# The layout of the attention output in HBM, and the tiles and queues of the first head's convolution

## The chip, the cores and the metric

The kernel runs on one core of one Trainium2 chip. The metric is the device time of one launch in microseconds (us). Three runs of the kernel before gave 3805.25, 3806.37 and 3806.59 us; the median is 3806.37. The trace and all rows quoted below come from one further, profiled execution.

The engines are called PE (TensorE), DVE (VectorE), ACT (ScalarE), POOL (GpSimd) and SP (SyncE). SP, ACT and POOL issue transfers, each in the order of its own instructions: SP and ACT through hardware queues (q1 and q10 in the profile), POOL through the software queue (q0).

## What is computed

Two layers over an image `x` of 48 channels and 256 by 256 pixels, in float32. Layer 0 is an attention over patches: 4 by 4 pixels are one token, so there are 4096 tokens (and a border of zero tokens), and each of 8 heads has 96 rows (6 channels of 16 pixels).

```python
def _L0_conv_ref(x, w_qkv, w_dw, temperature, w_proj):
    qkv = jnp.einsum('bchw,oc->bohw', x, w_qkv)
    qkv = dwconv3x3(qkv, w_dw)
    q, k, v = jnp.split(qkv, 3, axis=1)
    q, k, v = (heads(q), heads(k), heads(v))      # unfold into patches, 8 heads
    q = _l2norm(q)
    k = _l2norm(k)
    attn = jnp.einsum('bhcn,bhcm->bhnm', q, k) * temperature
    attn = jax.nn.softmax(attn, axis=-1)
    out = jnp.einsum('bhcn,bhnm->bhcm', v, attn)
    out = fold(out.reshape(b, -1, out.shape[-1]), h, w)
    return jnp.einsum('bchw,oc->bohw', out, w_proj)

x = x + _L0_conv_ref(_gn(x), ...)                 # _gn: normalisation over groups of channels
x = x + _L1_conv_ref(_gn(x), Ws, Hs, Cs, 64)      # three products over W, H and C in windows of 64 by 64
```

## The kernel before

The work runs in this order.

1. *Statistics and pointwise product.* `x` is read into 96 partitions (two halves of the image, 48 channels each), 16 rows at a time, by loads `xr` on SP and ACT. DVE takes statistics, PE forms q, k and v of the first two heads, and they go to HBM (`t1`).
2. *Convolution of the first head* (`depthwise_first`). The image is cut into ten rows of strips (`CR + 1`), and a `Depthwise` object does one of them for seven strips at once: 126 partitions (7 strips of 18 channels) by 4 rows of 256 pixels. The objects go in pairs: the second of a pair forms its taps on PE (L223), the first on DVE (L234). Then come square (ACT L245), sum (DVE L249), the sum over channels (PE L253), a root, the scaled result `o` (DVE L279), its high part `oh` (ACT L288) and the rest `ol` (POOL L292). `store` (L297) writes these three to `qkv` in HBM. One store has 504 KB: from each of 126 partitions 4 KB, to 16 rows of 256 bytes in HBM. All 30 are issued by POOL. The tiles come from a pool of two buffers each (`bufs` is 2), and the padded input `pad` from twice as many; `pad` loads are issued by SP. When a buffer is taken again, the instruction that writes it waits until the store that reads it has landed.
3. *Attention*, head by head, in an order written out by hand. First the eight key tiles of head 0 are loaded (`load_key`, L313), alternately from SP and ACT; a key tile of 512 columns takes four transfers, and eight where it crosses the border of a strip (576 columns). They wait for all stores of head 0's `qkv`. `scores` forms logits on PE (L339) into one of three `big` buffers of PSUM, ACT takes the exponential (L541), `weigh` multiplies with the values (L570) and DVE adds up `oacc`. The convolution of the next head runs beside it, one row for each group of queries. At the end of a head `store` (L590) turns the result by PE into `oo`, 96 rows by 512 tokens (two buffers), and POOL writes it into `os_`, which lies in HBM as 768 rows (48 channels by 16 places in the patch) of 4096 tokens.
4. *Projection.* It goes by eight tiles `t`, each of 256 tokens (16 image rows) in both halves of the image. For each half SP loads `pot` (L709), 48 partitions by 16 places by 256 tokens, and `pxt` (L710), the same pixels of `x`: four loads of 768 KB in the order pot, pxt, pot, pxt. PE multiplies with the projection weights (L715), DVE adds to `pxt` (L722) and takes statistics (L726), and POOL writes the sum to `x1s` in HBM (L731). The tiles have three buffers.
5. *Layer 1* reads `x1s` in windows and writes the output.

In step 2 the instructions of an engine are put in order by a scheduler; in step 3's loop they stand as written. The loads ahead of that loop:

```python
load_query(0, 0)
for m in range(NM):
    load_key(0, m, nc.scalar if m % 2 else nc.sync)
for m in range(2):
    load_value(0, m)
    turn(0, m)
```

Of the kernel before, what the change touches and what calls it, by code (L numbers as in the profile page):

```python
# [8 lines left out]
F32 = mybir.dt.float32  # L9
# [7 lines left out]
C = 48  # L17
# [3 lines left out]
KS = 4  # L21
KK = KS * KS
NH = 8
HD = C * KK // NH
NT = (H // KS) * (W // KS)
# [7 lines left out]
PX = W // KS  # L33
# [2 lines left out]
M1 = (NH - H0) * HC  # L36
GROUPS = [(0, H0), (H0, NH)]
NOT = 3
T3 = 3
WS = 64  # L40

# [2 lines left out]
def conv_preact_kernel(  # L44
# [15 lines left out]
    nc = tc.nc  # L60
# [4 lines left out]
    dram = ctx.enter_context(tc.tile_pool(name="dram", bufs=1, space=DRAM))  # L65
# [6 lines left out]
    CN = CR * PX  # L72
    t1 = [dram.tile([(h1 - h0) * HC, TR, W + 2], F32, name=f"t1_{h0}") for h0, h1 in GROUPS]
    qkv = [dram.tile([3, CH, HC * KK, CN + PX], F32, name=f"qkv{h}") for h in range(NH)]
    os_ = dram.tile([C * KK, NT], F32, name="os_")
    x1s = dram.tile([C, H, W], F32, name="x1s")


# [14 lines left out]
    for s in range(2):  # L93
        r = slice(s * C, (s + 1) * C)
        for h in range(NH if s == 0 else H0):
            o = s * M0 + h * HC if h < H0 else (h - H0) * HC
            nc.scalar.dma_start(
                out=(wq[r] if h < H0 else wr[0:C])[:, o : o + HC].rearrange("c (z e) -> c z e", z=3),
                in_=w_qkvT.rearrange("c (z h e) -> h c z e", z=3, h=NH)[h],
# [68 lines left out]
    class Strip:  # L168
# [24 lines left out]
        def store(self):  # L193
            for s, rows in enumerate(both_halves(t1[1], 2 * self.j, 2, base=1)):
                nc.sync.dma_start(out=rows, in_=self.ot[:, 2 * s : 2 * s + 2, :])

    class Depthwise:


        def __init__(self, h, r, pool=None):  # L200
            self.h, self.r = h, r
            self.pool, self.bufs = (pool, 2) if pool else (cv, 1)

        def load(self):
            g = [i for i, (h0, h1) in enumerate(GROUPS) if h0 <= self.h < h1][0]
# [85 lines left out]
            self.ol = self.pool.tile([NP1, KK, PX], F32R, name="ol", tag="t4", bufs=self.bufs)  # L291
            eng.tensor_sub(self.ol, self.o, self.oh.bitcast(F32))  # L292

        def store(self, parts=(0, 1, 2)):
            px = slice(self.r * PX, (self.r + 1) * PX)
            for i in parts:
                nc.gpsimd.dma_start(  # L297
                    out=qkv[self.h][i].rearrange("j (c k) n -> (j c) k n", k=KK)[:, :, px],
                    in_=self.o if i == 2 else (self.ol if i else self.oh).bitcast(F32),
                )  # L300
# [59 lines left out]
    def depthwise_first():  # L360

        with tc.tile_pool(name="dg", bufs=1) as dg, tc.tile_pool(name="dps", bufs=3, space=PSUM) as dps:
            diag = dg.tile([NP1, 9, NP1], F32, name="diag")
            for t in range(9):
                nc.gpsimd.tensor_scalar_mul(diag[:, t, :], ident[:NP1, :NP1], dwt[:, 0, t : t + 1])
            rows = [Depthwise(0, r, dg) for r in range(CR + 1)]
            for d in rows[:2]:
                d.load()
            for i in range(0, CR + 1, 2):
                a, b = rows[i : i + 2]  # L370
                b.taps_on_tensor(diag, dps.tile([NP1, 2, 512], F32, name="dps"))
                a.first()
                for t in range(1, 9):
                    a.tap(t)
                for d in rows[i + 2 : i + 4]:
                    d.load()
                for d in (a, b):
                    d.square()
                    d.reduce()
                    d.norm()  # L380
                    d.root(on_scalar=True)
                    d.scale()
                    d.high()
                    d.low(nc.gpsimd)
                    d.store()


    with tc.tile_pool(name="xn", bufs=1) as xnp, tc.tile_pool(name="cst", bufs=1) as cst, tc.tile_pool(
        name="nps", bufs=2, space=PSUM
# [9 lines left out]
        for j in range(0, HALF, LR):  # L399
            for s in range(2):  # L400
                eng = nc.sync if s == 0 else nc.scalar
                eng.dma_start(
                    out=xr[s * C : (s + 1) * C, j : j + LR, :], in_=xc[:, s * HALF + j : s * HALF + j + LR, :]
# [8 lines left out]
        for g, (w, k) in enumerate(((wq, P2), (wr, C))):  # L412
            m = w.shape[1]
# [31 lines left out]
        for y in range(0, HALF, OR):  # L445
            ot = xnp.tile([2 * M0, OR, W + 2], F32, name="ot0", bufs=4)
# [9 lines left out]
    cv = attention.enter_context(tc.tile_pool(name="cv", bufs=1))  # L456
# [8 lines left out]
    with tc.If(nc.values_load(large) > 0):  # L465
# [8 lines left out]
        with tc.tile_pool(name="mk", bufs=NM) as mk, tc.tile_pool(name="mq", bufs=2) as mq, tc.tile_pool(  # L474
            name="mps", bufs=2, space=PSUM
# [23 lines left out]
    with tc.tile_pool(name="ahead", bufs=2) as ah, tc.tile_pool(name="ae", bufs=3) as ae, tc.tile_pool(  # L499
        name="asm", bufs=6  # L500
# [6 lines left out]
        def load_key(h, m, eng=nc.sync):  # L507
            keys[h, m] = ah.tile([128, 2, 512], F32R, name="kt", bufs=14)
            load_keys(keys[h, m], h, m, eng)
# [73 lines left out]
        def store(h, m):  # L583

            pt = one.tile([HD, 4, 128], F32, name="pt", tag="one")
            for i in range(4):
                nc.tensor.transpose(pt[:, i, :], oaccs[h, m // 2][:, m % 2, i * HD : (i + 1) * HD], ident)  # L587
            oo = asm.tile([HD, 512], F32, name="oo", bufs=2)
            nc.scalar.copy(oo, pt.rearrange("p i n -> p (i n)"))  # L589
            nc.gpsimd.dma_start(out=os_[h * HD : (h + 1) * HD, m * 512 : (m + 1) * 512], in_=oo)  # L590

        load_query(0, 0)
        for m in range(NM):
            load_key(0, m, nc.scalar if m % 2 else nc.sync)
        for m in range(2):
            load_value(0, m)
            turn(0, m)
# [9 lines left out]
        with tc.manual_schedule():  # L607
            load_query(0, 1)
            block = scores(0, 0)
            for h in range(NH):  # L610
                more = h + 1 < NH
                rows = {r: Depthwise(h + 1, r) for r in range(CR + 1)} if more else {}
                for g in range(NG):
                    p, d, n = rows.get(g - 2), rows.get(g - 1), rows.get(g)
# [42 lines left out]
                    for k in range(NK):  # L657
                        s = (h * NG + g) * NK + k
# [33 lines left out]


    l1c = ctx.enter_context(tc.tile_pool(name="l1c", bufs=1))
    RP = 16
    NP = RP // KS * (W // KS)
    with tc.tile_pool(name="pj", bufs=3) as pj, tc.tile_pool(name="pjs", bufs=1) as pjs, tc.tile_pool(
        name="pps", bufs=3, space=PSUM
    ) as pps, tc.tile_pool(name="pp1", bufs=1, space=PSUM) as pp1:
        st1 = pjs.tile([P2, HALF * W // 512, 6], F32, name="st1")  # L700
        ov = os_.rearrange("(c k) n -> c k n", k=KK)
        for t in range(HALF // RP):
            ot = pj.tile([P2, KK, NP], F32, name="pot")
            xt = pj.tile([P2, RP, W], F32, name="pxt")
            for s in range(2):
                r = slice(s * C, (s + 1) * C)
                n0 = s * (NT // 2) + t * NP
                y0 = s * HALF + t * RP
                nc.sync.dma_start(out=ot[r], in_=ov[:, :, n0 : n0 + NP])  # L709
                nc.sync.dma_start(out=xt[r], in_=xc[:, y0 : y0 + RP, :])  # L710
            xv = xt.rearrange("p (py ki) (px kj) -> p ki kj py px", ki=KS, kj=KS)
            for ki in range(KS):
                ps = pps.tile([P2, KS, NP], F32, name="pps")
                for i in range(0, KS, 2):
                    nc.tensor.matmul(  # L715
                        ps[:, i : i + 2, :],
                        lhsT=wp,
                        rhs=ot[:, ki * KS + i : ki * KS + i + 2, :],
                        start=True,
                        stop=True,  # L720
                    )
                nc.vector.tensor_add(  # L722
                    xv[:, ki], ps.rearrange("p k (py px) -> p k py px", py=RP // KS), xv[:, ki]
                )
            for i in range(0, RP, 2):
                nc.vector.bn_stats(  # L726
                    st1[:, (t * RP + i) // 2, :], xt[:, i : i + 2, :].rearrange("p a b -> p (a b)")
                )
            for s in range(2):
                y0 = s * HALF + t * RP  # L730
                nc.gpsimd.dma_start(out=x1s[:, y0 : y0 + RP, :], in_=xt[s * C : (s + 1) * C])  # L731
# [202 lines left out]
```

## Time and profile before

| What | us |
|---|---|
| Median of three runs | 3806.37 |
| Profiled execution, whole time | 3807.91 |
| Its span, first to last instruction | 3806.1 |
| PE busy in it | 3512.4 (92%) |
| DVE busy | 2199.7 (58%) |
| ACT busy | 1718.5 (45%) |
| POOL busy | 584.2 (15%) |
| 0 to 152: statistics, pointwise product | 152 |
| 152 to 304: convolution of the first head, until its last store has landed | 152 |
| 304 to 330: first keys | 26 |
| 330 to 3305: attention | 2975 |
| 3305 to 3336: last group of head 7, first loads of the projection | 31 |
| 3336 to 3491: projection | 155 |
| 3491 to 3806: layer 1 | 315 |

Times of stages are counted from the span's start and are cut where the timeline shows the first or last instruction of the stage. Rows of a timeline have start, length, engine, line, operation and what it writes and reads, then in brackets the idle time before it and what ended it. A stage's share of DMA is the mean busy share of the core's 16 DMA engines.

### The profile page before, as it was taken

Reading aid. Unit: us, or ns where it says so; the run is one execution under the profiler, and the core shown is the slowest. Engines: PE = TensorE matmul, PEld = TensorE weight load, DVE = VectorE, ACT = ScalarE, POOL = GpSimd, SP = SyncE. Lnnn points to the kernel's source line nnn. Section 1 sums busy time; section 2 is a strip of 40 time slices with the busy share of each in tenths; the row PEclk is TensorE's granted clock in tenths of the full one; section 3 lists DMA queues with packets and bytes.
Section 4 is the critical chain, followed back from the end, with each engine's and each line's share of the span. In section 5 each row is a group of like instructions: output and inputs, shape, how many; then the busy total and the mean of one; then the engine's idle time right before and its main releaser. Section 6 shows DMA issues by size and latency. Waiting matters only on the chain.

```text
span 3806.1 us, 99864 instructions
## 1 busy us (share of the span) xinstructions
PE 3512.4 (92%) x44216; PEld 2911.7 (77%) x44216; DVE 2199.7 (58%) x3520; ACT 1718.5 (45%) x2668; POOL 584.2 (15%) x535
## 2 busy tenths in 40 slices
PE   1866999999999999999999999999999999854998
PEld 0224777788888888888888888888888888712776
DVE  4571776159826972896299439934992222265664
ACT  0223656555545554554455445545554444300232
POOL 0050122012201220122022102210220000000011
PEclk9887999999999999999999999999999999966999
DMA  7475676535433542344244424432443100299784
GB/s 137 153 164 148 177 194 185 173 111 127 108 86 94 127 116 74 104 122 109 84 106 120 98 83 114 119 98 76 123 115 92 41 19 19 47 233 187 126 145 90
DMA packets 280235, 441.66 MB, mean 116 GB/s; under 512 B 57354, under 2 KB 205082, under 8 KB 276336
## 3 DMA queue, kind: packets, MB, share of 16 engines
q1 hardware_dynamic: 225150, 260.52, 26.4%
q0 software_dynamic: 48896, 165.90, 19.4%
q10 hardware_dynamic: 5746, 8.73, 1.0%
q8 instruction: 351, 5.75, 0.6%
q14 instruction: 92, 0.75, 0.1%
HBM read 234.76 MB, written 199.95 MB: 114 GB/s over the span
## 4 chain that ended last, share of the span: by engine, by line
PE 74%; issue 11%; DMA 6%; SPq 1%; DVE 0%; POOL 0%; ACT 0%; POOLq 0%; ACTq 0%
PE big L339 32%; PE big L570 31%; PE pb L832 4%; PE pa L810 2%; PE pc L849 2%; PE big L183 2%; DMA pot<-os__70 1%; DMA pxt<-in_x_dram 1%; PE pst L524 1%; PE pt L587 1%; PE pn L253 1%; DMA x1s<-pxt 1%; DMA t<-ot 1%; DMA kt<-qkv 1%; DMA lxq<-x1s 0%
## 5 line engine op out<-in xcount | busy, mean ns | idle before, releaser
L541 ACT ACTIVATE e<-big,nmx 128x1024 f32<-128x1024 f32 x1024 | 1144.4, 1118 | 843.3 <-PE big L339 634.3
L339 PE MATMUL big<-kt,qt 128*128 128x512 f32 x6144 | 1443.1, 394 | 56.8 <-DMA kt<-qkv 54.5
L570 PEld LDWEIGHTS big<-vn,e 128*64 128x64 f32 x32768 | 1364.6, 137 | 87.8 <-ACT e L541 45.1
L570 PE MATMUL big<-vn,e 128*64 128x96 f32 x32768 | 1422.3, 247 | 9.2 <-ACT ot L186 4.0
L339 PEld LDWEIGHTS big<-kt,qt 128*128 128x128 f32 x6144 | 1147.5, 189 | 322.1 <-issue 62.3
L581 DVE TENSOR_TENSOR oacc<-big,oacc 128x768 f32<-128x768 f32 x480 | 458.0, 954 | 707.7 <-PE big L570 707.7
L234 DVE SCALAR_TENSOR_TENSOR acc<-pad,dwt,acc 126x1024 f32<-126x1024 f32 x600 | 779.2, 1300 | 34.0 <-ACT acc L215 18.2
L292 POOL TENSOR_TENSOR ol<-o,oh 126x1024 fp32r<-126x1024 f32 x80 | 190.1, 2376 | 908.3 <-DVE ss L249 808.7
L554 DVE TENSOR_REDUCE zt<-zs 128x1 f32<-128x4 f32 x256 | 38.9, 152 | 367.9 <-ACT e L541 367.9
L541 ACT ACTIVATION_READ_ACCUMULATOR e<-big,nmx 128x1 f32 x1024 | 196.0, 191 | 0.0
L817 DVE TENSOR_TENSOR lzt<-pa,cbias 128x864 f32<-128x864 f32 (+1 forms) x88 | 136.9, 1626 | 99.7 <-PE pa L810 99.7
L297 POOL DMA_DIRECT2D qkv<-o x80 | 101.1, 1264 | 565.7 <-DVE zu L556 339.9
L839 ACT COPY lyt<-pb 128x512 f32<-128x512 f32 x144 | 84.5, 586 | 215.7 <-PE pb L832 215.7
L245 ACT ACTIVATE sq<-acc 126x1024 f32<-126x1024 f32 x75 | 79.3, 1058 | 172.2 <-issue 111.7
L279 DVE TENSOR_TENSOR o<-acc,y 126x1024 f32<-126x1024 f32 x75 | 149.5, 1993 | 10.5 <-DMA qkv<-o 10.5
L832 PEld LDWEIGHTS pb<-wsb,lzt 128*64 128x64 f32 x2304 | 125.8, 138 | 28.4 <-issue 20.3
L715 PE MATMUL pps<-pot,wp 96*96 96x512 f32 x128 | 80.2, 797 | 71.4 <-DMA pot<-os__70 71.4
L832 PE MATMUL pb<-wsb,lzt 128*64 128x128 f32 x2304 | 141.8, 279 | 1.9 <-issue 1.9
L186 ACT ACTIVATE ot<-big,bias 108x1024 f32<-108x1024 f32 x64 | 71.1, 1113 | 145.6 <-PE big L183 76.9
L590 POOL DMA_DIRECT2D os__70<-oo x64 | 32.7, 516 | 616.5 <-ACT oo L589 616.4
L715 PEld LDWEIGHTS pps<-pot,wp 96*96 96x96 f32 x128 | 27.2, 220 | 123.8 <-issue 116.2
L215 ACT ACTIVATE acc<-pad,dwt 126x1024 f32<-126x1024 f32 x75 | 85.3, 1137 | 72.7 <-DMA pad<-t 72.7
(115 smaller groups left out, 1888.7 us busy)
## 6 DMA issues: line engine op xcount, KB each, us to landing
pad<-t SPq DMA_DIRECT2D x80, 761.9 KB
qkv<-o POOLq DMA_DIRECT2D x80, 504.0 KB, 7.0
qkv<-oh POOLq DMA_DIRECT2D x80, 504.0 KB, 7.4
qkv<-ol POOLq DMA_DIRECT2D x80, 504.0 KB, 9.1
t<-ot SPq DMA_DIRECT2D x128, 217.7 KB
qt<-qkv SPq DMA_DIRECT2D x176, 96.0 KB
xs<-in_x_dram SPq DMA_DIRECT2D x128, 96.0 KB
os__70<-oo POOLq DMA_DIRECT2D x64, 192.0 KB, 2.9
```

The source lines that it names most:

```text
L215: nc.scalar.mul(self.acc, self.pad[:, 0:KS, 0:W], dwt[:, self.h, 0:1])
L234: nc.vector.scalar_tensor_tensor(self.acc, self.pad[:, dy : dy + KS, dx : dx + W], dwt[:, self.h, tap : tap + 1], self.acc, ALU.mult, ALU.add,
L279: nc.vector.tensor_tensor(self.o.rearrange("p (a b) x -> p a b x", a=KS), self.acc.rearrange("p a (x b) -> p a b x", b=KS), self.y.rearran ...
L292: eng.tensor_sub(self.ol, self.o, self.oh.bitcast(F32))
L297: nc.gpsimd.dma_start(out=qkv[self.h][i].rearrange("j (c k) n -> (j c) k n", k=KK)[:, :, px], in_=self.o if i == 2 else (self.ol if i else ...
L339: nc.tensor.matmul(ps[:, i, :], lhsT=qt[:, r, q0 : q0 + 128], rhs=kts[2 * j + i][:, r // 2, :], start=(r == 0), stop=(r == 2),)
L541: nc.scalar.activation(e[:, j * 1024 : (j + 1) * 1024], ps.rearrange("p a b -> p (a b)"), AF.Exp, bias=nmx[:, b : b + 1], accum_out=zs[:, ...
L570: nc.tensor.matmul(ps[p : p + 64, j // 4, j % 4 * HD : (j % 4 + 1) * HD], lhsT=e[:, mb * 128 + p : mb * 128 + p + 64], rhs=vn, start=(i == 0),
L581: nc.vector.tensor_add(oaccs[h, k], ps[:, :, : 4 * HD], oaccs[h, k])
L715: nc.tensor.matmul(ps[:, i : i + 2, :], lhsT=wp, rhs=ot[:, ki * KS + i : ki * KS + i + 2, :], start=True, stop=True,)
L817: nc.vector.tensor_tensor(zv[:, :, y0 : y0 + n, :], pa[:, :, : n * T3 * C].rearrange("p s (y k) -> p s y k", y=n), cbias.rearrange("p (u v ...
L832: nc.tensor.matmul(pb[s * WS : (s + 1) * WS, i, :], lhsT=zts[u][:, t * C + c + i, :], rhs=wsb[:, t, :], start=True, stop=True,)
```

## The change

It has three parts. First, `os_` gets another layout: 16 blocks of 256 tokens, each holding all 768 rows, so that what one `pot` load reads is one block without gaps. The stores of the attention output are cut in two to match, and `RP` and `NP` are now written in terms of the block's size, with the same values (16 and 256). Second, the first head's convolution takes four buffers of each tile (and eight of `pad`), and the stores of `oh` and `o` are issued by SP, that of `ol` by POOL. Third, which the short description leaves out, the eight key tiles of head 0 are loaded in turn from ACT, SP and POOL.

```diff
--- before.py
+++ after.py
@@ -36,6 +36,7 @@
 M1 = (NH - H0) * HC
 GROUPS = [(0, H0), (H0, NH)]
 NOT = 3
+TP = 256
 T3 = 3
 WS = 64
 
@@ -72,7 +73,8 @@
     CN = CR * PX
     t1 = [dram.tile([(h1 - h0) * HC, TR, W + 2], F32, name=f"t1_{h0}") for h0, h1 in GROUPS]
     qkv = [dram.tile([3, CH, HC * KK, CN + PX], F32, name=f"qkv{h}") for h in range(NH)]
-    os_ = dram.tile([C * KK, NT], F32, name="os_")
+
+    os_ = dram.tile([NT // TP, C * KK, TP], F32, name="os_")
     x1s = dram.tile([C, H, W], F32, name="x1s")
 
 
@@ -199,7 +201,7 @@
 
         def __init__(self, h, r, pool=None):
             self.h, self.r = h, r
-            self.pool, self.bufs = (pool, 2) if pool else (cv, 1)
+            self.pool, self.bufs = (pool, 4) if pool else (cv, 1)
 
         def load(self):
             g = [i for i, (h0, h1) in enumerate(GROUPS) if h0 <= self.h < h1][0]
@@ -291,10 +293,10 @@
             self.ol = self.pool.tile([NP1, KK, PX], F32R, name="ol", tag="t4", bufs=self.bufs)
             eng.tensor_sub(self.ol, self.o, self.oh.bitcast(F32))
 
-        def store(self, parts=(0, 1, 2)):
+        def store(self, parts=(0, 1, 2), eng=nc.gpsimd):
             px = slice(self.r * PX, (self.r + 1) * PX)
             for i in parts:
-                nc.gpsimd.dma_start(
+                eng.dma_start(
                     out=qkv[self.h][i].rearrange("j (c k) n -> (j c) k n", k=KK)[:, :, px],
                     in_=self.o if i == 2 else (self.ol if i else self.oh).bitcast(F32),
                 )
@@ -381,8 +383,10 @@
                     d.root(on_scalar=True)
                     d.scale()
                     d.high()
+                    d.store((0,), nc.sync)
                     d.low(nc.gpsimd)
-                    d.store()
+                    d.store((1,))
+                    d.store((2,), nc.sync)
 
 
     with tc.tile_pool(name="xn", bufs=1) as xnp, tc.tile_pool(name="cst", bufs=1) as cst, tc.tile_pool(
@@ -587,11 +591,14 @@
                 nc.tensor.transpose(pt[:, i, :], oaccs[h, m // 2][:, m % 2, i * HD : (i + 1) * HD], ident)
             oo = asm.tile([HD, 512], F32, name="oo", bufs=2)
             nc.scalar.copy(oo, pt.rearrange("p i n -> p (i n)"))
-            nc.gpsimd.dma_start(out=os_[h * HD : (h + 1) * HD, m * 512 : (m + 1) * 512], in_=oo)
+            for i in range(512 // TP):
+                nc.gpsimd.dma_start(
+                    out=os_[m * (512 // TP) + i, h * HD : (h + 1) * HD, :], in_=oo[:, i * TP : (i + 1) * TP]
+                )
 
         load_query(0, 0)
         for m in range(NM):
-            load_key(0, m, nc.scalar if m % 2 else nc.sync)
+            load_key(0, m, (nc.scalar, nc.sync, nc.gpsimd)[m % 3])
         for m in range(2):
             load_value(0, m)
             turn(0, m)
@@ -692,21 +699,20 @@
 
 
     l1c = ctx.enter_context(tc.tile_pool(name="l1c", bufs=1))
-    RP = 16
-    NP = RP // KS * (W // KS)
+    RP = TP // PX * KS
+    NP = TP
     with tc.tile_pool(name="pj", bufs=3) as pj, tc.tile_pool(name="pjs", bufs=1) as pjs, tc.tile_pool(
         name="pps", bufs=3, space=PSUM
     ) as pps, tc.tile_pool(name="pp1", bufs=1, space=PSUM) as pp1:
         st1 = pjs.tile([P2, HALF * W // 512, 6], F32, name="st1")
-        ov = os_.rearrange("(c k) n -> c k n", k=KK)
+        ov = os_.rearrange("t (c k) n -> t c k n", k=KK)
         for t in range(HALF // RP):
             ot = pj.tile([P2, KK, NP], F32, name="pot")
             xt = pj.tile([P2, RP, W], F32, name="pxt")
             for s in range(2):
                 r = slice(s * C, (s + 1) * C)
-                n0 = s * (NT // 2) + t * NP
                 y0 = s * HALF + t * RP
-                nc.sync.dma_start(out=ot[r], in_=ov[:, :, n0 : n0 + NP])
+                nc.sync.dma_start(out=ot[r], in_=ov[s * (NT // 2 // TP) + t])
                 nc.sync.dma_start(out=xt[r], in_=xc[:, y0 : y0 + RP, :])
             xv = xt.rearrange("p (py ki) (px kj) -> p ki kj py px", ki=KS, kj=KS)
             for ki in range(KS):
```

On SP all ten `pad` loads stand ahead of the 20 new stores. On DVE some scaled results `o` move ahead of or behind a few taps; the numbers of instructions of PE, DVE and ACT other than loads are the same.

## The prediction

> **What bounds the kernel now.** I read the page first: PE is busy 92% of the span, in two slices of the forty it is down to 4 and 5 tenths, and the first two are nearly empty. No edit touches the attention heads, where PE is full, so I cut the span into stages (busy time by stage) and looked at those where PE is not. Columns: stage, length, then busy time of PE, PEld, DVE, ACT and POOL, the PE clock, the DMA share, GB/s.
>
> ```profile
> 190.00:266.00 76.00, 61.53 (x144) 26.97 (x142) 67.61 (x64) 19.84 (x26) 43.10 (x28) 0.92 0.70 168
> 266.00:304.00 38.00, 0.00 (x0) 0.00 (x0) 3.27 (x3) 3.94 (x5) 18.06 (x12) 0.50 0.75 151
> 304.00:330.00 26.00, 12.02 (x21) 5.94 (x22) 0.00 (x0) 3.40 (x6) 0.00 (x0) 0.50 0.66 191
> 1140.00:3305.00 2165.00, 2162.11 (x29512) 1918.18 (x29508) 1278.74 (x2250) 1117.04 (x1766) 336.75 (x268) 1.00 0.36 91
> 3336.00:3491.00 155.00, 81.62 (x134) 28.46 (x134) 102.84 (x102) 0.20 (x1) 8.25 (x16) 0.68 0.97 223
> ```
>
> The first row is the first head's convolution: DVE sets its pace (67.6 of 76 us). The second is its end: no engine works, DMA does. The third is the loading of the first keys. The last is the projection: the DMA engines are 97% busy, DVE only 103 of 155 us, so that stage is DMA's. Head stages (fourth row) are PE's and stay as they are.
>
> Next the timeline of DVE and the chain of waits at the end of the convolution, and the timeline of the queues at the keys:
>
> ```profile
> 276.62 1.98 DVE L279 TENSOR_TENSOR o<-acc,y 126x1024 f32<-126x1024 f32 x1 [10.54 <-DMA qkv<-o]
> 284.27 1.22 DVE L279 TENSOR_TENSOR o<-dps,y 126x1024 f32<-126x1024 f32 x1 [5.68 <-DMA qkv<-o]
> ...
> 291.20 12.19 DMA qkv<-o
> ...
> 306.75 20.23 SPq L313 DMA_DIRECT2D kt<-qkv  x28
> ...
> 303.69 22.37 ACTq L313 DMA_DIRECT2D kt<-qkv  x28
> 326.10 1.11 ACT L541 ACTIVATE e<-big,nmx 128x1024 f32<-128x1024 f32 x1 [31.54 <-DMA kt<-qkv]
> ```
>
> Rows 8 and 9 could be scaled at 266.1 and wait until 276.6 and 284.3 for the stores of rows 6 and 7 to release `o`. The last store lands at 303.4; only then do the key loads start. ACT's first exp stands behind ACT's 28 key loads, and PE has only three `big` buffers until ACT reads one.
>
> Last the DMA view of the projection (3317 to 3482; packets, MB, share of 16 engines) and who waits for `pot`:
>
> ```profile
> q1 hardware_dynamic: 13440, 23.59, 75.9%
> q0 software_dynamic: 1284, 12.20, 19.4%
> ...
> L715 PE MATMUL pps<-pot,wp 96*96 96x512 f32 x128 | 80.2, 797 | 71.4 <-DMA pot<-os__70 71.4
> ```
>
> The packet records of the trace, sorted by queue and size, split q1 there into 12,288 packets of 1 KB (`pot`: mean 93 ns, 1137 us of engine time) and 672 of 16 KB (`pxt`: mean 1274 ns, 856 us); q0 is `x1s`, 16 KB at 657 ns.
>
> [...] These stores write 256 B rows; no 256 B write on a hardware queue is in this trace. [...] `xr` (48 partitions, 16 KB packets) takes 1.35 us a packet, 12 GB/s an engine; `pad` on 126 partitions 26 GB/s (6.2 KB in 236 ns).
>
> **Part A, output by tiles of the projection.** Each `pot` load becomes 48 runs of 16 KB instead of 768 of 1 KB; bytes are the same. Nearest row: `pxt`, same shape on the same partitions, 1.274 us. 768 packets x 1.274 = 978 us against 1137, that is 159/16 = 10 us of all engines. Better end: [...] if the source side limited, as `pad` runs without it (16 KB in about 0.65 us), 500 us, 40 us; [...] so I cap at 30. Worse end: the 1 KB packets ran at 1.49 us per 16 KB, so equal bytes at equal rate give 0. As `pot` packets also slow their neighbours (`pxt` of the first half has 1.65 us, of the second 1.0), I take -14, from 0 to -30. DVE's 102.8 us is the next limit, about 50 us further down. Writing: 128 stores of 96 KB instead of 64 of 192 KB. Each costs POOL 0.51 us; the 112 of heads 0 to 6 lie beside a full PE and an idle POOL (337 of 2165 us). In the last head `oo` (two buffers) is released by the second store, twice in a row: +1 us on the path into the projection.
>
> **Part B, four tiles each and stores over two queues.** DVE: the two waits, 10.5 and 5.7 us, go; rows 8 and 9 are scaled by 269.3. `pad` gets eight buffers: all loads except two are issued at once, ahead of every store on SP, so no store delays them. POOL loses 20 of 30 issues, 1.14 us apart, all off the path. What is late next is DMA. Rows 5 to 7, nine stores, took it from 252 to 279: 3.0 us a store. It then idled about 4 us until rows 8 and 9 came at 282. Without the stall, the 15 stores from 252 on take 45 us, to 297, plus a landing of 1 to 2 us: -5. This holds if an SP store costs the same. Its price is not in the trace. Hardware packets from HBM take 18 ns at 256 B, 27 at 512, 46 at 1 KB, so 9 ns a packet and 9 per 256 B; the software queue writes 16 rows of 256 B in one 4 KB packet at 195 ns (median) to 311 (full queue), 12 to 19 ns a row. An SP row is then 18 to 28 ns: 2016 x 18/14 engines = 2.6 us, x 28 = 4.0 us. At 2.6 the stage ends at 293 (-10); at 4.0, 20 x 4.0 + 10 x 3.0 = 110 us from 190, near 302 (-1). I take 3.2 us and -5, from -10 to +12[...]. The waiting SP stores block only later stores: key and query loads on SP need all of them landed anyway.
>
> **Part C, keys over three queues.** Key tiles cross the 576-column strips, so the eight take 4,8,8,8,8,8,8,4 issues. Before: 28 on SP, 28 on ACT. After: ACT tiles 0, 3, 6, 20 issues; SP 1, 4, 7, 20 issues; POOL 2, 5, 16 issues, at 0.53 us each as POOL's later key loads show. ACT: 22.37/28 = 0.80 us each, 16.0 us, done 6.4 us sooner. SP: 20.23/28 = 0.72, 14.5 us, 5.8 sooner; the values, strip inputs and queries behind them on SP move up with it. POOL 9 us. Nothing of POOL's is held up, its next store comes after the first group. The 4 MB then have some 20 us: 210 GB/s, while this stage already shows 230 for stretches, so part may be lost to transfer: -5, from -7 to -1. Tile 1 comes later (behind six query loads on SP), which costs nothing as PE needs the last tile for its first block anyway. The first head after it waits on SP and moves as a whole.
>
> **Sum.** -14 + 1 - 5 - 5 = -23 us. The profiled execution, 3806.1 us of span and 3807.9 in all, becomes 3783 and 3785; the median of the runs shown (3806.4) lies 1.5 us below the profiled one, so I forecast 3783.
>
> **Rivals.**
> - *The projection doesn't move* (chance 0.17): [...] 16 KB packets bring nothing. For it: `xr`, 16 KB throughout, is as slow. Against: `pot` is slower per byte than `pxt` beside it. A = 0: 3797.
> - *The source side was the limit* (0.17): strided rows of `os_` were slow to read. For it: 1 KB packets of `kt` take 46 ns, of `pot` 93. Against: `kt` loads go beside one another to 96, 32 and 64 partitions[...]. A = -30: 3767.
> - *Slower: 256 B writes on SP* (0.11): if they cost 50 ns a row, a store takes 7.2 us on 14 engines; 20 of them and 10 on POOL need 174 us from 190, so the keys start at 364, not 304: +60 - 13 - 5 = +42, 3848. It decides from about 35 ns (5.0 us a store, end at 321, which eats the other 18 us). Against: the 195 ns for sixteen such rows on POOL's queue. For: nothing in the trace has this form.
> - *Nothing arrives* (0.08): [...] a full DMA at the keys, and stores at 4 us: A -3, B 0, C -1: 3803.
>
> **How the numbers follow.** Likeliest case 0.47 with its own range 3775 to 3792. A measurement of this kernel can tell about 0.2%, 8 us. Likeliest and fast-source cases lie below 3798, and most of the first rival does at 3797: faster 0.78, same 0.11, slower 0.11. Range 3760 to 3800: it takes in the fast source case almost whole and the unmoved projection, and leaves out the slow stores.
>
> **What would show it.** Right: q1 in the projection has about 1,500 data packets and the stage is 10 to 20 us shorter; no wait of DVE L279 on `qkv<-o`; the last `qkv` store lands near 298 and ACT's first exp comes some 16 us after the key loads start. Wrong: 16 KB `pot` packets at 1.5 us or more; SP `qkv` packets above 30 ns and key loads that start after 304; PE's first matmul block ending no sooner after the last store than before (27 us).

## The result, and the profile after

Four runs of the changed kernel gave 3774.44 to 3789.12 us, median 3779.85; four of the kernel before, on the same chip, 3805.25 to 3809.05, median 3806.48. The ratio is 0.9932, with a 95% interval of 0.9911 to 0.9952: about 26 us less. The profiled execution has a span of 3787.3 us (3789.12 in all), 18.8 us less than the one before; it is the longest of its four.

The first view is the busy time by stage. Columns: stage, length, busy time of PE, PEld, DVE, ACT and POOL, the PE clock, the DMA share, GB/s.

```profile
190.00:266.00 76.00, 60.58 (x143) 26.71 (x141) 68.91 (x62) 19.73 (x26) 29.09 (x16) 0.94 0.78 176
266.00:290.00 24.00, 0.00 (x0) 0.00 (x0) 3.21 (x4) 3.79 (x4) 7.19 (x4) 0.50 0.71 151
290.00:316.00 26.00, 12.85 (x41) 8.26 (x42) 0.48 (x3) 5.65 (x10) 8.17 (x16) 0.65 0.78 210
...
3322.00:3472.00 150.00, 78.68 (x134) 27.40 (x132) 102.14 (x102) 0.20 (x1) 8.25 (x16) 0.68 0.92 229
```

The stretch between the last tap and the keys (second row) had 38 us and now has 24. In it no engine is the limit, as before. While DVE still works (first row) the DMA engines are busier than they were, 78% instead of 70%, and POOL has 29 us of work instead of 43. In the projection the DMA share has fallen from 0.97 to 0.92, but the engines are not idler. The share adds up the packets' times, and packets overlap in the record: counted at each moment, up to 23 packets were under way on the 16 engines before, up to 20 after. Between the first and the last product of the loop (143.5 us before, 139.1 after) the engines' idle time is 5% in both kernels, nearly all of it in the last tenth, where few loads are left; in the first eight tenths all 16 are busy without a break. The stage is still DMA's.

At the end of the convolution, from the timelines of DVE, SP and ACT (start, length, engine, line, operation, what it writes and reads, in brackets the idle time before it):

```profile
265.24 1.97 DVE L281 TENSOR_TENSOR o<-acc,y 126x1024 f32<-126x1024 f32 x1
...
268.11 1.23 DVE L281 TENSOR_TENSOR o<-dps,y 126x1024 f32<-126x1024 f32 x1
```

```profile
274.57 6.29 SPq L299 DMA_DIRECT2D qkv<-o  x1
...
293.05 17.78 SPq L315 DMA_DIRECT2D kt<-qkv  x20
```

```profile
289.85 19.70 ACTq L315 DMA_DIRECT2D kt<-qkv  x19
309.59 1.11 ACT L545 ACTIVATE e<-big,nmx 128x1024 f32<-128x1024 f32 x1 [33.28 <-DMA kt<-qkv]
```

Both waits of DVE for the stores of `o` (10.54 and 5.68 us) are gone. The key loads, which wait for all stores, start at 289.4 instead of 303.7. ACT issues fewer of them (20 instead of 28), but they take it nearly as long, and its first exp comes 20 us after their start.

To compare launches I count the stages from the records of the instructions, and the convolution from the first tap on DVE, since the stage ahead of it varies by itself (the first tap lies between 155.4 and 162.7 us in these launches). All times in us:

| Stage | before | after | after, second launch |
|---|---|---|---|
| start to first tap | 160.5 | 160.1 | 155.4 |
| first tap to first key load | 143.2 | 129.3 | 130.1 |
| key loads to end of the first group of queries | 61.2 | 56.8 | 59.0 |
| rest of the first head | 419.1 | 424.4 | 418.4 |
| end of head 7 to first projection product | 12.4 | 13.5 | 10.9 |
| projection loop | 152.7 | 148.4 | 142.2 |
| span | 3806.1 | 3787.3 | 3769.3 |

The second launch is from a later set of runs of the same kernel (`e10_again`). The gain sits in the convolution, the keys and the projection; the rest of the first head takes back 5 us in one launch and nothing in the other.

### The profile page after: what moved, and what is told of

The parts are those of the page before. It is cut to its first block, busy times and chain, and to the rows that moved or that the text cites. A ratio compares the mean times of both kernels' runs of the same rounds, so it can differ in the third digit from the quotient of the medians.

```text
span 3787.3 us, 99981 instructions
## 1 busy us (share of the span) xinstructions
PE 3511.2 (93%) x44216; PEld 2913.1 (77%) x44216; DVE 2201.6 (58%) x3520; ACT 1719.0 (45%) x2668; POOL 599.8 (16%) x595
## 4 chain that ended last, share of the span: by engine, by line
PE 82%; DMA 6%; issue 2%; DVE 1%; SPq 1%; ACT 0%; POOL 0%; ACTq 0%; POOLq 0%
PE big L341 36%; PE big L574 35%; PE pb L838 4%; PE pa L816 2%; PE pc L855 2%; PE big L185 1%; DMA pad<-t 1%; DMA x1s<-pxt 1%; PE pt L591 1%; PE pst L528 1%; DMA pxt<-in_x_dram 1%; DMA pot<-os__70 1%; DMA t<-ot 1%; PE pn L255 1%; DMA qkv<-ol 0%
## 5 line engine op out<-in xcount | busy, mean ns | idle before, releaser
L299 POOL DMA_DIRECT2D qkv<-o x70 | 86.1, 1231 | 511.0 <-DVE zu L560 243.6
L595 POOL DMA_DIRECT2D os__70<-oo x128 | 65.1, 515 | 594.0 <-ACT oo L593 593.6
L217 ACT ACTIVATE acc<-pad,dwt 126x1024 f32<-126x1024 f32 x75 | 85.3, 1137 | 73.3 <-DMA pad<-t 73.3
```

What stands on the lines that cost most here:

```text
L217: nc.scalar.mul(self.acc, self.pad[:, 0:KS, 0:W], dwt[:, self.h, 0:1])
L299: eng.dma_start(out=qkv[self.h][i].rearrange("j (c k) n -> (j c) k n", k=KK)[:, :, px], in_=self.o if i == 2 else (self.ol if i else self. ...
```

## The experiments

Each kernel ran beside the kernel before on the same chip (medians of the latter 3803 to 3806 us). "Before" or "after" says which kernel the edit starts from.

**One part at a time.** The first three kernels hold one part of the change each.

The layout alone (`e1_layout`), the changed kernel with the other two parts undone:

```diff
-            self.pool, self.bufs = (pool, 4) if pool else (cv, 1)
+            self.pool, self.bufs = (pool, 2) if pool else (cv, 1)
...
-                    d.store((0,), nc.sync)
                     d.low(nc.gpsimd)
-                    d.store((1,))
-                    d.store((2,), nc.sync)
+                    d.store()
...
-            load_key(0, m, (nc.scalar, nc.sync, nc.gpsimd)[m % 3])
+            load_key(0, m, nc.scalar if m % 2 else nc.sync)
```

> Part A alone: the attention output by tiles of the projection, nothing else. Theory (what the trace of the changed kernel says): a 16 KB packet into 48 partitions is nearly as slow as sixteen of 1 KB, so the projection shortens by 4 to 6 us, the start of it comes 1 us later, and the whole is 3 to 5 us faster than before (ratio about 0.999); q1 packets of pot 1.1 to 1.3 us. Rival 1, the prediction's own step: 13 us faster (ratio 0.9965); its loss in the full kernel came from what it meets there. Rival 2: nothing, within 2 us. The convolution's last store lands at about 303 as before in all three.

Measured: 3797.15 us, ratio 0.9970 [0.9959, 0.9982]. The first tap to the keys takes 143.0 us, as before; the projection loop takes 143.3, 9 us less. That is the prediction's own size (Rival 1), not the 3 to 5 us expected here.

Tiles and queues alone (`e2_conv`), the kernel before with:

```diff
-            self.pool, self.bufs = (pool, 2) if pool else (cv, 1)
+            self.pool, self.bufs = (pool, 4) if pool else (cv, 1)
...
+                    d.store((0,), nc.sync)
                     d.low(nc.gpsimd)
-                    d.store()
+                    d.store((1,))
+                    d.store((2,), nc.sync)
```

> Part B alone: four tiles each, eight pads, stores of o and oh on SP. Theory: the last store of the first head lands at about 289.5 instead of 303.4, and the first head's attention keeps 8 to 14 of those 14 us; ratio 0.9965 to 0.998. Rival, the prediction's step: 5 us (ratio 0.9987), and what the changed kernel showed beyond it came from the layout or the key loads. Keys still take 22 us of issue on ACT, so first exp is about 22.4 us after the key loads start.

Measured: 3790.88 us, 0.9960 [0.9943, 0.9977]. First tap to keys 131.7 us: 11.5 less.

The keys over three queues alone (`e3_keys`), the kernel before with:

```diff
-            load_key(0, m, nc.scalar if m % 2 else nc.sync)
+            load_key(0, m, (nc.scalar, nc.sync, nc.gpsimd)[m % 3])
```

> Part C alone: first keys over three queues. Theory: as predicted, the first exp comes 16 to 20 us after the key loads start (22.4 before), the end of the first group of queries 4 to 6 us sooner, and the whole 3 to 5 us faster (ratio about 0.999) unless the first head's SP queue gives it back. Rival: transfers bound, no gain, ratio 1.000.

Measured: 3800.09 us, 0.9986 [0.9977, 0.9996]. First exp 20.3 us after the key loads start (22.4 before), first group of queries done after 56.9 (61.2 before).

In thousandths the three parts make 3.0 + 4.0 + 1.4 = 8.4 (32 us), the whole change 6.8 and, in the later set of runs, 8.4. The parts add up within the intervals.

**The tiles or the queue?** The middle part has two edits. `e4_tiles4` has only the first line of the diff of `e2_conv` (four buffers, eight of `pad`, all stores on POOL), `e5_queues` only the other lines (two queues, two buffers), and `e6_pad8` the kernel before with eight `pad` buffers and nothing else:

```diff
-            self.pad = self.pool.tile([NP1, KS + 2, W + 2], F32, name="pad", bufs=2 * self.bufs)
+            self.pad = self.pool.tile([NP1, KS + 2, W + 2], F32, name="pad", bufs=4 * self.bufs if self.bufs > 1 else 2)
```

> Half of part B: four tiles each and eight pads, all 30 stores still on POOL. Theory (buffers): the gain of the convolution is that of the buffers: the two waits of DVE on o go, and pads load ahead of the stores into idle DMA time (4 pads, about 4 us of all engines); last store lands at 290 to 293. Rival (queues): one queue can't keep the engines filled; last store lands at 297 to 300 and the rest needs the second queue.

> The other half of part B: stores of o and oh on SP, that of ol on POOL, but two tiles each and four pads as before. Four tiles alone brought the start of the key loads to 298.6, both together to 291. Theory (feeding): the second queue helps because o and oh are issued as soon as they are there, not behind POOL's subtraction and two other issues, while a store costs the engines the same; with two tiles DVE still waits for the release of o, so the key loads start at 293 to 297. Rival (buffers needed for it): without free tiles the second queue has nothing to issue earlier, 301 to 304.

> The pads alone: eight buffers of the padded input, two of all other tiles, all stores on POOL. It moves four loads of 762 KB ahead of 190 us, where the engines were a third busy; these take some 4 us of all engines. Theory: little, because the end of this stage is set by the wait for o: key loads start at 300 to 304, time within 3 us of before. Rival (DMA work): what leaves the crowded stretch shortens it, 297 to 300, 4 us faster.

Measured:

| Kernel | us | ratio [95%] | first tap to last `o` | to last store issued | to first key load |
|---|---|---|---|---|---|
| before | | | 123.7 | 130.7 | 143.2 |
| `e4_tiles4` | 3800.91 | 0.9986 [0.9977, 0.9996] | 111.5 | 122.3 | 139.0 |
| `e5_queues` | 3792.88 | 0.9970 [0.9958, 0.9981] | 111.8 | 116.9 | 129.6 |
| `e6_pad8` | 3800.59 | 0.9992 [0.9978, 1.0007] | | | 143.5 |
| after | 3779.85 | 0.9932 [0.9911, 0.9952] | 108.0 | 115.0 | 129.3 |

Four tiles alone take away DVE's waits, and the last `o` comes 12 us sooner, but the keys only 4 us. The second queue with two tiles has one wait left and brings the keys 13.6 us forward, as much as the whole change. So the tiles were not needed for it (`e2_conv`, with both, has 131.7 from the first tap to the keys), and the eight `pad` bring nothing that can be told from no change. The end of the two kernels on DVE, first `e4_tiles4`, then `e5_queues`:

```profile
271.09 1.22 DVE L279 TENSOR_TENSOR o<-dps,y 126x1024 f32<-126x1024 f32 x1
```

```profile
261.28 1.97 DVE L279 TENSOR_TENSOR o<-acc,y 126x1024 f32<-126x1024 f32 x1
...
267.50 1.23 DVE L279 TENSOR_TENSOR o<-dps,y 126x1024 f32<-126x1024 f32 x1 [3.44 <-DMA qkv<-o]
```

The last `o` comes at the same time in the two (111.5 and 111.8 us after the first tap), yet the keys start 9.4 us apart. What differs is how full the DMA engines are before that. The busy time in the stretches from 30 to 112 us and from 112 to 129 us after the first tap, for the kernel before, `e4_tiles4`, `e5_queues` and the changed kernel in this order (the last two columns are the DMA share and GB/s):

```profile
190.50:272.50 82.00, 61.03 (x142) 26.74 (x140) 67.26 (x62) 19.49 (x26) 48.62 (x32) 0.89 0.72 168
272.50:289.50 17.00, 0.00 (x0) 0.00 (x0) 3.20 (x2) 2.09 (x2) 8.86 (x6) 0.50 0.72 143
```

```profile
189.60:271.60 82.00, 63.00 (x143) 27.90 (x141) 75.10 (x64) 20.67 (x27) 48.53 (x33) 0.91 0.73 155
271.60:288.60 17.00, 0.00 (x0) 0.00 (x0) 0.71 (x1) 2.75 (x3) 11.84 (x8) 0.50 0.92 176
```

```profile
185.70:267.70 82.00, 60.94 (x143) 27.01 (x141) 71.08 (x65) 20.76 (x27) 31.93 (x18) 0.87 0.82 193
267.70:284.70 17.00, 0.00 (x0) 0.00 (x0) 1.03 (x1) 2.74 (x3) 4.26 (x3) 0.50 0.79 170
```

```profile
190.10:272.10 82.00, 60.48 (x143) 26.61 (x141) 72.04 (x64) 21.72 (x28) 32.41 (x18) 0.91 0.78 174
272.10:289.10 17.00, 0.00 (x0) 0.00 (x0) 0.00 (x0) 1.70 (x2) 3.87 (x3) 0.50 0.76 163
```

With all stores on POOL, behind its subtractions, the DMA engines are 72 to 73% busy while DVE works, with or without more tiles. In `e4_tiles4` a backlog of stores is left when DVE is done, and the engines are then 92% busy with it: there DMA is the limit, but because it was fed too late. With the second queue the share in the long stretch is 78 to 82%, and the stores move 12.7 to 12.8 MB in it instead of 11.0 before and 11.4 in `e4_tiles4`, by the packet records. Why POOL feeds late is seen on its timeline in `e4_tiles4`:

```profile
255.22 2.62 POOL L292 TENSOR_TENSOR ol<-o,oh 126x1024 fp32r<-126x1024 f32 x1 [9.42 <-ACT oh L288]
257.79 1.23 POOL L297 DMA_DIRECT2D qkv<-oh  x1
258.92 1.34 POOL L297 DMA_DIRECT2D qkv<-ol  x1
260.04 1.50 POOL L297 DMA_DIRECT2D qkv<-o  x1
261.19 2.72 POOL L292 TENSOR_TENSOR ol<-o,oh 126x1024 fp32r<-126x1024 f32 x1
263.48 1.62 POOL L297 DMA_DIRECT2D qkv<-oh  x1
264.62 1.74 POOL L297 DMA_DIRECT2D qkv<-ol  x1
265.73 1.88 POOL L297 DMA_DIRECT2D qkv<-o  x1
```

`oh` is there at 255.2, but POOL first subtracts, and its store goes out 2.6 us later; the second row stands behind the first row's three issues. From the first subtraction to the last issue of the pair 12.4 us pass, after 9.4 us in which POOL had nothing. On SP no subtraction stands between the stores, though they do not all leave as soon as their tile is there. The last stores of the changed kernel on SP, ahead of the one at 274.57 shown above:

```profile
267.23 2.12 SPq L299 DMA_DIRECT2D qkv<-o  x1
269.45 5.03 SPq L299 DMA_DIRECT2D qkv<-oh  x2
```

The first of these starts as `o` is ready (267.21), the last store of `o`, ready at 269.34, only at 274.57, behind SP's own issues. One such issue took SP between 0.8 and 13.4 us in this stage; what it waits for is not shown. SP has nothing else to do meanwhile.

**Is one software queue enough without the subtraction?** `e12_no_low`, the kernel before with four tiles, without the first head's subtraction (`oh` is stored in the place of `ol`, so 30 stores stay):

```diff
-                    d.low(nc.gpsimd)
-                    d.store()
+                    d.store((2,))
+                    d.ol = d.oh
+                    d.store((0, 1))
```

> Four tiles each, all 30 stores on POOL, but the subtraction that forms ol left out in the first head (the high part is stored a second time in its place, so that part of the computation is changed; the bytes are the same). It tells what held four tiles alone back (139.0 us from the first tap on DVE to the first key load; 129.6 with the second queue alone). Theory (POOL's own time): its subtractions, 2.35 us each between the stores, delay the issues; without them POOL issues the last store at 117 us or sooner and the key loads start at 129 to 133 us. Rival (one software queue is slower than two queues): 137 to 140 us as before.

Measured: 3785.41 us, 0.9952 [0.9925, 0.9980]; first tap to keys 129.5 us, with every store on POOL. The same two stretches:

```profile
189.90:271.90 82.00, 58.17 (x142) 25.63 (x140) 59.58 (x64) 23.32 (x30) 35.06 (x29) 0.87 0.87 185
271.90:288.90 17.00, 0.00 (x0) 0.00 (x0) 0.00 (x0) 0.00 (x0) 1.38 (x2) 0.50 0.49 110
```

So a second queue is not needed as such to bring the keys this early. But two things went at once here. DVE also does its 64 instructions in 59.6 us instead of 75.1, and the last `o` comes at 97.2 instead of 111.5. One group of DVE shows what POOL's subtraction does to it (min, median and max ns), in the kernel before (the maximum of `e4_tiles4` is 4833) and in `e12_no_low`:

```profile
L234 DVE SCALAR_TENSOR_TENSOR acc<-pad,dwt,acc x600: 1184/1285/4837, 160.5 to 2842.1; 126x1024 f32<-126x1024 f32 x150
```

```profile
L234 DVE SCALAR_TENSOR_TENSOR acc<-pad,dwt,acc x600: 1186/1285/1287, 159.9 to 2824.5; 126x1024 f32<-126x1024 f32 x150
```

How much of the gain of `e12_no_low` is POOL's earlier issue and how much DVE's earlier `o` is therefore not separated. The last `o` comes 11 us sooner than in the changed kernel (97.2 and 108.0), yet the keys start at the same time (129.5 and 129.3): what DVE gains is lost again in the stores. Of POOL's last issues some wait for earlier stores to land, the last goes out at 112.6, and in the last 17 us the engines are 49% busy:

```profile
266.30 1.22 POOL L297 DMA_DIRECT2D qkv<-oh  x1 [4.20 <-DMA qkv<-oh]
269.53 1.22 POOL L297 DMA_DIRECT2D qkv<-o  x1 [2.00 <-DMA qkv<-oh]
```

**What limits the projection.** Two edits of the changed kernel. `e7_xblocks` reads `pxt` from 768 KB of `x` in one piece instead of 48 strided rows, so the residual takes other pixels; `e8_halves` lets ACT issue the loads of the second half:

```diff
-                nc.sync.dma_start(out=xt[r], in_=xc[:, y0 : y0 + RP, :])
+                n0 = (2 * t + s) * C * RP * W
+                nc.sync.dma_start(
+                    out=xt[r].rearrange("p a b -> p (a b)"),
+                    in_=xc.rearrange("c y x -> (c y x)")[n0 : n0 + C * RP * W].rearrange("(p f) -> p f", p=C),
+                )
```

```diff
+                eng = nc.scalar if s else nc.sync
-                nc.sync.dma_start(out=ot[r], in_=ov[s * (NT // 2 // TP) + t])
-                nc.sync.dma_start(out=xt[r], in_=xc[:, y0 : y0 + RP, :])
+                eng.dma_start(out=ot[r], in_=ov[s * (NT // 2 // TP) + t])
+                eng.dma_start(out=xt[r], in_=xc[:, y0 : y0 + RP, :])
```

> The changed kernel, with pxt read from x in blocks of 768 KB without gaps (16 KB to each of 48 partitions, as before, but one behind the other in HBM): the residual then takes other pixels of x, so that part of the computation is changed. It tells whether the 256 KB step between channels makes these packets slow. Theory (receiving partitions): [...] packets stay at 1.1 to 1.3 us and the projection at 143 to 149 us. Rival (source): packets of 16 KB fall to 0.8 us or less and the projection shortens by 15 us or more.

> The changed kernel, with the loads of the second image half (partitions 48 to 95) of the projection issued by ACT, those of the first by SP, so that both halves are under way at the same time. Theory (receiving partitions): [...] the mean rate of loads rises and the projection shortens by 8 to 20 us. Rival (all 16 engines are simply full): the same bytes in the same time, within 3 us of 143 to 149.

Measured: `e7_xblocks` 3780.21 us, 0.9924 [0.9902, 0.9946]; `e8_halves` 3783.33, 0.9940 [0.9920, 0.9961]. Neither differs from the changed kernel beyond the intervals. All packets of the projection's loads and writes, sorted by queue and size:

| Kernel | `pot`, ns | `pxt`, ns | `x1s`, ns |
|---|---|---|---|
| before | 12,288 of 1 KB at 93 | 16 KB at 1291 | 16 KB at 704 |
| `e1_layout` | 16 KB, both together 1164 | | 805 |
| after | 16 KB, both together 1200 | | 828 |
| `e7_xblocks` | 16 KB, both together 1167 | | 791 |
| `e8_halves` | 16 KB, SP's 1190, ACT's 1153 | | 715 |

Sources without any stride leave the packets as they were (1167 ns against 1200 and 1164), so the stride on the side of HBM is not their limit. Halves on two queues do not speed them up either (1190 and 1153 ns). In `e8_halves` the loop is shorter (121 us), but it starts 20 us later: ACT and SP send six loads of `pxt` ahead, and ACT's next copy into `oo` waits 19.23 us for a store of `oo` to land, which takes 2.2 us from its issue at the median of the changed kernel:

```profile
3310.28 0.58 ACT L593 COPY oo<-pt 96x512 f32<-96x512 f32 x1 [19.23 <-DMA os__70<-oo]
```

From the end of head 7 to the end of the loop it has 153.6 us, against 155.4 in `e1_layout`, 161.9 and 153.1 in two launches of the changed kernel and 165.1 before.

**Does the first head give the keys' gain back?** In the changed kernel's trace the rest of the first head took 5 us more than before, and a theory was that the third queue pushes strip loads together. `e9_no_third` is the changed kernel with the key loads on two queues again (the last lines of the diff of `e1_layout`), `e10_again` the changed kernel once more, and `e11_pads_pool` lets POOL issue the `pad` loads during the heads:

```diff
-        def load(self):
+        def load(self, eng=nc.sync):
...
-                        rows[0].load()
+                        rows[0].load(nc.gpsimd)
...
-                            rows[g + 1].load()
+                            rows[g + 1].load(nc.gpsimd)
```

> The changed kernel without the third queue for the first keys (parts A and B alone). Alone, part C brings the end of the first group of queries forward by 4 us; in the three profiles with all parts the first head after that group takes 420 to 424 us against 414 to 419 in the others, with pad loads of 17 to 19 us on the chain of waits. Theory (given back): without C the first group ends 4 us later, but the first head takes 414 to 419 us, so the time is within 3 us of the changed kernel's. Rival (part C pays in full): 4 to 5 us slower than the changed kernel, first head 420 us or more as well.

> The changed kernel once more, for more runs of its time beside the kernel before on the same chip, and a second profile. Expected: ratio 0.993 to 0.995; from the first tap on DVE to the first key load 129 to 131 us; first head 420 to 424 us; projection loop 143 to 149 us.

> The changed kernel with the pad loads of the attention heads issued by POOL instead of SP, a version that might beat both. Theory: in the first head SP stands still when a pad load has not landed, as its semaphore is needed again, and strip loads behind it come late for PE; without pads on SP the first head loses its two long groups: 408 to 415 us, 6 to 12 us faster than the changed kernel. Rival: the transfers themselves are too many for that stretch, the waits move to other loads, first head 418 to 424 us.

Measured, all on one chip:

| Kernel | us | ratio [95%] | keys to first group's end | rest of first head |
|---|---|---|---|---|
| `e9_no_third` | 3776.97 | 0.9930 [0.9909, 0.9952] | 61.5 | 417.0 |
| `e10_again` | 3772.88 | 0.9916 [0.9894, 0.9938] | 59.0 | 418.4 |
| `e11_pads_pool` | 3770.78 | 0.9920 [0.9898, 0.9942] | 58.3 | 416.8 |

The same kernel has 424.4 in one launch and 418.4 in another: the 5 us belong to the launch. In the first one the chain of waits shows where they are:

```profile
423.56 18.03 DMA pad<-t
...
448.55 7.27 DMA xs<-in_x_dram
```

The second launch has no such wait for `pad`, and a similar one for other loads (11.50 and 11.21 us for `vt`). So this stretch of one launch is no evidence for the theory. Over all traces it does not fall, though: the rest of the first head takes 419.8 us on average with the third queue (six traces, 416.8 to 424.4) and 416.6 without it (eight, 413.8 to 419.1), so most of what the keys gain is missing again at the end of the head. `e9_no_third` has the 417.0 us of the theory and is 4.1 us slower than `e10_again` beside it, as the rival said, but the intervals of the two overlap. Whether the third queue shows in the whole time beside the other parts is not decided. In the first launch of the changed kernel SP waited for `pad` loads to land six times between 316 and 761 us, 16.6 us in all, ahead of loads of keys, queries and values. `e11_pads_pool` takes `pad` off the chain of waits and gets values (12.10 us), queries (9.61) and strips (12.67) there; it is not told apart from the changed kernel. Its expected 6 to 12 us did not come. No run is clearly faster than the changed kernel.

## Why the prediction was right, and where it was not

The forecast of 3783 us lay within the range of the runs. Its parts, against what was measured:

- *Part A, -14 with +1 at its start:* The loads got cheaper as sized. Before, they needed 1137 + 991 us of engine time; in the changed kernel 1,536 packets of 1200 ns make 1843. That is 285 us less, or 18 us of 16 engines, since the neighbours sped up too. But the loop became only 4 us shorter in that trace, and 9 us on average (143.8 over six traces with the new layout, `e8_halves` left out, 152.5 over seven with the old); the 0.9970 of `e1_layout` is 11 us. The step "159/16 = 10 us of all engines", with the 4 us for the neighbours, was too high by two terms that the sum left at nothing. The writes of `x1s` beside them (16 of 48 packets) went from 704 to 828 ns a packet, which gives back 768 x 124 / 16 = 6 us. And packet times that overlap can't all be saved: before, their sum exceeds the time in which engines were busy by 5% of the loop, after by 1%, so some 6 of the 18 us had been counted twice. What is left, 18 - 6 - 6 = 6 us, is near the 4 of that trace. The +1 at the start can't be told from the spread (10.9 to 13.5 us after, 11.2 to 13.8 before).
- *What limits a 16 KB packet:* With the new layout these packets took 1.15 to 1.20 us on average (table above), whatever the source, near the 1.274 us of `pxt` from which the prediction sized its -10. What limits them is not shown. The loads had on average 11 of the 16 engines, and in the loop of the changed kernel they moved 1,309 x 16 KB in 139.1 us, 154 GB/s. The rival that the source side is the limit falls: `pot` without gaps in HBM did not become faster than that in `e1_layout`, nor `pxt` in `e7_xblocks`. The one in which the projection doesn't move falls with `e1_layout`.
- *Part B, -5:* measured -11.5 alone and -13.9 in the whole change. The removed DVE waits were read rightly, and removing them alone gets 4 us (`e4_tiles4`), but most of what held the keys was something else. The step that failed reads "POOL loses 20 of 30 issues, 1.14 us apart, all off the path", and with it "What is late next is DMA ... 3.0 us a store". The 3.0 us between stores came from rows fed late by POOL, not from DMA's price: 30 stores take 1182 us of engine time before, 1182/30/16 = 2.5 us each, and 2.4 after. Those issues, behind POOL's subtractions, were on the path: `e4_tiles4` and `e5_queues` have the last `o` at the same time, and the one in which SP has 20 of them starts the keys 9.4 us sooner. The second issuer did not make a store cheaper for the DMA engines (38.4 us of engine time on SP's queue, 39 on POOL's). What it saved is the wait behind the work that POOL has in front, here 9 us from `e4_tiles4` to `e5_queues` and 14 from the kernel before.
- *Price of an SP store:* within the bounds (18 to 28 ns a row): 40,320 packets at 19 ns on average, 38.4 us of engine time a store, where the software queue needs 39. No record names the engine of a packet. The 14 engines by which the prediction divides are an estimate that the counts of the changed kernel's trace bear: one semaphore update comes within 0.5 us of the end of an SP store's issue and 14 follow later; for a `pad` load it is one and 7, and from 152 to 189 us, where `pad` loads run alone, seven of their packets are under way in 32.4 of the 36.4 us in which any is. The rival of slow 256-byte writes, from 35 ns on, did not happen.
- *Part C, -5:* -4 as the mean over traces (61.5 without it, 57.8 with it), 5 us in the ratio of `e3_keys`. But the first exp came 20 us after the key loads start, not 16. The term "16.0 us" took 0.80 us for each of ACT's 20 issues; they took 20.27 us in `e3_keys`, that is 1.0 us each, hardly less in all than the 28 before. PE's first block of logits was still done sooner, 24.2 us after the start of the key loads instead of 27.8. The step "the first head after it ... moves as a whole" is not borne out: without the third queue the rest of that head is 3 us shorter on average.
- *The sum:* A was too large by 3 to 5 us and B too small by 7 to 9; that -23 fits 26 well is in part two errors that cancel.

Open: how the gain of `e12_no_low` divides between POOL's issues and the hold of POOL's subtraction on DVE; how much of part C's gain the rest of the first head gives back; and what limits a 16 KB packet in the projection.

## What to carry to other kernels

Before a gap between transfers is priced as DMA's, compare it with the engine time of its packets (here 3.0 us between stores that cost 2.5): if the engines are not full (here 72%), look at what stands ahead of the issue on the issuer's engine. Here the stores were better issued by SP, which had nothing to compute: the keys came 13.6 us sooner with it, and 4 us sooner with four buffers alone, which moved the wait from DVE to POOL's issues. In a stage where transfers take all the time, as in the projection, a cheaper load paid only in part: the writes of `x1s` beside it went from 704 to 828 ns a packet, and of the 18 us saved in packet times some 6 had been counted twice, as packets overlap.

## What the runs showed that was not expected

DVE's instructions are held while POOL subtracts. In `e4_tiles4` a short DVE instruction that takes 0.30 us elsewhere took 2.36 us beside POOL's subtraction of 255.22 to 257.84 and ended with it:

```profile
250.66 0.30 DVE L262 TENSOR_SCALAR y<-y,nmul,nadd 126x64 f32<-126x64 f32 x1
...
255.53 2.36 DVE L262 TENSOR_SCALAR y<-y,nmul,nadd 126x64 f32<-126x64 f32 x1
```

The taps are held longer still. The longest, in the kernel before, took 4.84 us instead of 1.29:

```profile
194.72 4.84 DVE L234 SCALAR_TENSOR_TENSOR acc<-pad,dwt,acc 126x1024 f32<-126x1024 f32 x1
```

```profile
195.79 2.68 POOL L292 TENSOR_TENSOR ol<-o,oh 126x1024 fp32r<-126x1024 f32 x1
```

It began 1.07 us ahead of the subtraction and ended 1.09 us after it. All nine taps of over 1.5 us in the traces of the kernel before (five) and of the changed kernel (four) ended 1.08 to 1.09 us after a subtraction, nearly a whole tap, whenever they had begun. The longest was held although it began first, but POOL was already issuing a store then (194.64 to 196.09). Whether that counts, and by what DVE is held, no run shows. The other order occurs too: where POOL had been idle, a tap from 247.34 to 248.62 kept its length, and the subtraction that began within it took 3.04 us instead of 2.35. In the first head of the kernel before five taps are held, 10 us of DVE in all, and DVE sets the pace there.

The engine time of the 256-byte rows, 19 ns on the hardware queue, was not expected either: one packet a row there, one of 4 KB for sixteen rows on the software queue, at 293 ns or 18 ns a row. And launches of one kernel differ, by the stage ahead of the first tap and by waits for loads in the first head: the two spans of the changed kernel are 3787.3 and 3769.3 us, and 54 runs of the kernel before lie between 3786.88 and 3820.24, so that the 5 us of `e3_keys` took 22 runs to be seen.
